# Output stores and residual rows on GpSimd's queue, and the largest magnitude in one reduction, in a gated cross-attention kernel

## The chip, the cores and the metric

The kernel runs on one core of a Trainium2 chip. The metric is the device time of one execution in microseconds (us). Five engines work beside each other, each through its own instructions in order: TensorE (PE, with its weight loads PEld), VectorE (DVE), ScalarE (ACT), GpSimd (POOL) and SyncE (SP), which here only issues transfers. A transfer (DMA) is issued from an engine's queue, and everything behind it in that queue waits until it has been issued.

## The reference

Four stages are applied to x of 2 x 2048 tokens with 512 values each: a cross attention to 128 context rows, a routed block over 256 chosen tokens per batch entry, a second cross attention, and a feed-forward with quantized weights and activations. The change lies in the last:

```python
x = x + jnp.tanh(g_ffn[1]) * _L1_ffn_ref(_layernorm(x, axis=-1), L1_ffn_w1, L1_ffn_conv_w, L1_ffn_conv_b, L1_ffn_w2)

def act_quant(x):
    scale = 127.0 / jnp.clip(jnp.max(jnp.abs(x), axis=-1, keepdims=True), 1e-05)
    return jnp.clip(jnp.round(x * scale), -128, 127) / scale
...
h = bit_linear(x, w1)                             # 512 -> 2048, both sides quantized
h = depthwise_conv1d(h.transpose(0, 2, 1), conv_w, conv_b)   # 3 taps over the tokens
h = jax.nn.silu(h.transpose(0, 2, 1))
return bit_linear(h, w2)                          # 2048 -> 512, both sides quantized
```

The inner rows h need the largest magnitude of each token over all 2048 channels before any of them can be quantized.

## The kernel before, in words

The 4096 tokens are worked on in eight blocks of 512 (`g` from 0 to 7, `LAST` is 7); a block's inner rows are 16 chunks (`HC`) of 128 channels by 512 tokens.

**Stage 3 and the first half.** The second cross attention (`cross_attention`, lines L119 to L131 for the softmax, L253 for queries, L276 scores, L294 and L295 transposes, L302 values, L320 the output product and L329 its addition) runs block after block. When a block is done, `stage3_done` stores its rows (`x3_d`, L1284) and appends two generators to `stream`: `quantize_rows` (integers of the 512 inputs; L90 on POOL gives its normalisation) and `first_half`. `beside4` advances them a few steps beside each of the next block's units. `first_half` works in four groups of four chunks: `convolved` multiplies (L1157), scales (L1167) and convolves a chunk (L1169 on ACT, L1173 twice on DVE). The two columns that the next block needs are copied in and out on POOL (L1166, L1168). Then the group of 128x2048 goes through Silu (L1198), is stored to `h_d` (L1204, SP's queue), and its largest magnitudes are taken: absolute value on ACT in place (L1205), then maxima on DVE (L1206, L1210, L1211, in a block's first group L1206 and L1208). Block 7 is kept on the chip, so its group is not stored, and its absolute values go to a tile of their own (L1202). Blocks 0 to 3 are quantized early (`integers`, L1249 to L1263) and stored as integers in `hq_d`.

**The second half** starts at the end of stage 3 (`second_half_starts`: the weights `w2q`, L1325; integers of blocks 0 and 1; first residual rows). For each block, four tiles of 128 tokens go through `down_and_out`: 16 matmuls into one of four accumulators (L1386), the addition to the residual row tile (L1389, DVE) and the output store (L1390, SP). `row_tile` loads a residual row tile one block ahead (L1316, L1318, SP; eight tiles). `quantize_hidden(g + 1)` runs beside block `g`: for blocks 0 to 3 it loads integers (L1346), for 4 to 6 it loads inner rows (L1353, SP, eight buffers, six chunks ahead), multiplies them by their scale (L1362, DVE) and rounds them on ACT (L1365, L1366) or DVE (L1368). Integer tiles come from two pools, of which the second, `act5`, lies in memory that stage 3 holds until its last product (L320). `last_tokens` handles the final token of each batch entry, whose convolution ends at the border: some small steps and 32 matmuls of one column, called ahead of block 6's rows.

The order of each queue is fixed when the kernel is built, by a scheduler that goes by the order of the program text, ready times and its own estimates; SP's loads, stores and row loads are therefore mixed, but once built their order stands.

Of the kernel before, what the change touches and what calls it, by code (L numbers as in the profile page):

```python
# [10 lines left out]
F32 = mybir.dt.float32  # L11
BF16 = mybir.dt.bfloat16
AF = mybir.ActivationFunctionType
ALU = mybir.AluOpType
AX = mybir.AxisListType
PSUM = bass.MemoryType.PSUM

P = 128
# [3 lines left out]
BLK = 512  # L22
TB = BLK // P
NBLK = S // BLK
# [8 lines left out]
HC = HID // P  # L33
# [10 lines left out]
def flamingo_kernel(ctx: ExitStack, tc: tile.TileContext, a: dict, out: bass.AP):  # L44
    nc = tc.nc
# [697 lines left out]
    with ExitStack() as st:  # L743
# [16 lines left out]
            out=pick,  # L760
            in_=pick,
# [10 lines left out]
            out=after,  # L772
            in_=after,
# [301 lines left out]
    GC = 4  # L1075
# [8 lines left out]
    LAST = B * NBLK - 1  # L1084
# [65 lines left out]
    carry, ending, kept, act5 = {}, [], [], []  # L1150

    def convolved(g, c, z):

        cr = carry[g // NBLK]
        ph = ps_mm.tile([P, BLK], F32, name="ph", tag="mm")
        for d in range(DC):
            nc.tensor.matmul(  # L1157
                ph,
                w1q[:, d, ts(c, P)],
                xiT[g][:, d, :],  # L1160
                start=(d == 0),
                stop=(d == DC - 1),
            )

        u = act4.tile([P, BLK + 2], F32, name="u", tag="u", bufs=3)
        nc.gpsimd.tensor_copy(u[:, 0:2], cr[:, c, :])  # L1166
        nc.vector.tensor_tensor(u[:, 2:], ph, inv_b[g], ALU.mult)  # L1167
        nc.gpsimd.tensor_copy(cr[:, c, :], u[:, BLK:])  # L1168
        nc.scalar.activation(  # L1169
            z, u[:, 1 : BLK + 1], AF.Identity, scale=cw[:, c, 1:2], bias=cb[:, c : c + 1]  # L1170
        )
        for k in (0, 2):
            nc.vector.scalar_tensor_tensor(  # L1173
                z, u[:, ds(k, BLK)], cw[:, c, k : k + 1], z, ALU.mult, ALU.add
            )

    def first_half(g):

        if g % NBLK == 0:

            carry[g // NBLK] = act4.tile([P, HC, 2], F32, name="carry", tag="carry")
            nc.gpsimd.memset(carry[g // NBLK], 0.0)
        amax = act4.tile([P, BLK], F32, name="amax", tag="amax", bufs=1)
        for k in range(HC // GC):
            def hidden(pool, **kw):
                return pool.tile([P, GC, BLK], F32, **kw)

            if g == LAST and k == HC // GC - 1:
                h = hidden(act5[0], name="h7", tag="h7")
            else:  # L1190
                h = hidden(act4, name="h", tag="h", bufs=3)
            if g == LAST:
                kept.append(h)
            for c in range(GC):
                convolved(g, k * GC + c, h[:, c, :])
                if c < GC - 1:
                    yield
            nc.scalar.activation(h, h, AF.Silu)  # L1198

            if g == LAST:  # L1200
                z, h = h, hidden(act5[0], name="ab", tag="ab")
                nc.scalar.activation(h, z, AF.Abs)  # L1202
            else:
                nc.sync.dma_start(out=h_d[g][:, ts(k, GC), :], in_=h)  # L1204
                nc.scalar.activation(h, h, AF.Abs)  # L1205
            nc.vector.tensor_tensor(h[:, 0:2, :], h[:, 0:2, :], h[:, 2:4, :], ALU.max)  # L1206
            if k == 0:
                nc.vector.tensor_tensor(amax, h[:, 0, :], h[:, 1, :], ALU.max)  # L1208
            else:
                nc.vector.tensor_tensor(h[:, 0, :], h[:, 0, :], h[:, 1, :], ALU.max)  # L1210
                nc.vector.tensor_tensor(amax, amax, h[:, 0, :], ALU.max)  # L1211
            yield
        ending.append(scales_of(g, amax))
        if g % NBLK == NBLK - 1:
            b = g // NBLK
            tap = row4.tile([P, HC], F32, name="tap", tag="tap")
            nc.vector.tensor_tensor(tap, carry[b][:, :, 0], cw[:, :, 0], ALU.mult)
            nc.vector.tensor_tensor(z_last[:, b, :], carry[b][:, :, 1], cw[:, :, 1], ALU.mult)
            nc.vector.tensor_tensor(z_last[:, b, :], z_last[:, b, :], tap, ALU.add)
            nc.vector.tensor_tensor(z_last[:, b, :], z_last[:, b, :], cb, ALU.add)  # L1220
# [88 lines left out]
    def row_tile(g, i):  # L1309

        t = w5[0].tile([P, D], F32, name="x5w", tag="x5w", bufs=2)
        if g * TB + i > 1:
            t = act5[0].tile([P, D], F32, name="x5", tag="x5", bufs=8)
        r, p = g % NBLK * BLK + i * P - 1, 0
        if r < 0:
            nc.sync.dma_start(out=t[0:1, :], in_=x3_d[g // NBLK][0:1, :])  # L1316
            r, p = 0, 1
        nc.sync.dma_start(out=t[p:, :], in_=x3_d[g // NBLK][ds(r, P - p), :])  # L1318
        return t, r, p

    def second_half_starts():
# [10 lines left out]
    def quantize_hidden(g):  # L1332

        hq[g] = []

        def integer_tile():

            pool, bufs = (w5[0], 12) if next(next_integers) % 24 < 12 else (act5[0], 12)
            hq[g].append(pool.tile([P, GQ, BLK], BF16, name="hq", tag="hq", bufs=bufs))
            return hq[g][-1]  # L1340

        if g < EARLY:
            for k in range(HC // GQ):
                if g == 1 and k == HC // GQ // 2:
                    yield
                nc.sync.dma_start(out=integer_tile(), in_=hq_d[g][:, ts(k, GQ), :])  # L1346
            return

        def load(c):
            if g == LAST:  # L1350
                return kept[c // GC][:, c % GC, :]
            h = xr.tile([P, D], F32, name="x3", tag="x3")
            nc.sync.dma_start(out=h, in_=h_d[g][:, c, :])  # L1353
            return h

        AHEAD = 6
        hs = [load(c) for c in range(AHEAD)]
        s_b = scales_spread(g)
        yield
        for c in range(HC):  # L1360
            h = hs.pop(0)
            nc.vector.tensor_tensor(h, h, s_b, ALU.mult)  # L1362
            q = (integer_tile() if c % GQ == 0 else hq[g][-1])[:, c % GQ, :]
            if c % 4:
                nc.scalar.activation(h, h, AF.Copy, bias=RND)  # L1365
                nc.scalar.activation(q, h, AF.Copy, bias=-RND)  # L1366
            else:
                nc.vector.tensor_scalar(q, h, RND, RND, ALU.add, ALU.subtract)  # L1368
            if c + AHEAD < HC:
                hs.append(load(c + AHEAD))  # L1370
            if c % 2:
                yield
# [6 lines left out]
    act5.append(s4.enter_context(tc.tile_pool(name="act5", bufs=1)))  # L1379
    w2q = w5[1]  # L1380

    def down_and_out(rows, col, n, t, to, p=0):

        po = ps_5[0].tile([n, D], F32, name="po4", tag="o4")
        for c in range(HC):
            nc.tensor.matmul(  # L1386
                po, rows(c), w2q[:, c, :], start=(c == 0), stop=(c == HC - 1)
            )
        nc.vector.scalar_tensor_tensor(t, po, col, t, ALU.mult, ALU.add)  # L1389
        nc.sync.dma_start(out=to, in_=t[p:, :])  # L1390

    def last_tokens():

# [4 lines left out]
        pm = ps_mm.tile([P, B, P], F32, name="pml", tag="mm")  # L1398
        for b in range(B):
            nc.tensor.transpose(pm[:, b, :], own[:, b : b + 1].to_broadcast([P, P]), ident)  # L1400
        m = row4.tile([P, B], F32, name="ml", tag="lm")
        nc.vector.tensor_reduce(m, pm, AX.X, ALU.max)
        nc.vector.tensor_scalar(m, m, 1e-5, None, ALU.max)
# [7 lines left out]
        for b in range(B):  # L1411
            nc.vector.tensor_scalar(h[:, b, :], h[:, b, :], s[:, b : b + 1], None, ALU.mult)
        nc.vector.tensor_scalar(q, h, RND, RND, ALU.add, ALU.subtract)
        for b in range(B):
            t = act5[0].tile([P, D], F32, name="x5", tag="x5", bufs=8)[0:1, :]
            nc.sync.dma_start(out=t, in_=x3_d[b][S - 1 : S, :])
            down_and_out(
                lambda c: q[:, b, c : c + 1],
                fin[0:1, b : b + 1],
                1,  # L1420
                t,
                out[(b + 1) * S - 1 : (b + 1) * S, :],
            )
# [4 lines left out]
    for g in range(LAST + 1):  # L1428
        if g == LAST - 1:
            while stream or ending:  # L1430
                beside4(None)
            last_tokens()
        behind = quantizing[1] if g == 0 else quantize_hidden(g + 1) if g < LAST else iter(())
        for i in range(TB):
            t, r, p = ahead.pop(0)
            down_and_out(
                lambda c: hq[g][c // GQ][:, c % GQ, ts(i, P)],
                hid_f[:, g * TB + i : g * TB + i + 1],
                P,
                t,  # L1440
                out[ds(g // NBLK * S + r, P - p), :],
                p,
            )
            if g < LAST:
                ahead.append(row_tile(g + 1, i))
            for _ in range(3):
                next(behind, None)
                beside4(None, 1)
# [65 lines left out]
```

## Time and profile before

| | |
|---|---|
| median of 3 runs | 1804.85 us (1802.63 to 1807.84) |
| profiled execution | 1800.29 us, span 1798.6 us |
| mean granted TensorE clock | 0.967 |
| second half, 1600 to 1798.6 us | PE busy 167.7, DVE 145.4, ACT 108.0, POOL 21.3 us |
| stores of inner rows (L1204) | 28 of 1024 KB |
| loads of inner rows in the second half (L1353) | 48 of 256 KB |
| loads of integers (L1346) | 32 of 256 KB |

The profile is taken on one execution. Busy times of an engine are the union of its instructions; a row of costly groups gives a line, its engine, output and inputs, shapes and count, then busy us and mean ns of one, then the engine's idle time just before and what ended most of it. The chain is followed back from the last instruction to whatever released each step.

### The profile page before, as it was taken

To read this page: it belongs to the slowest core of one execution; us is meant where nothing else is said; L and a number is where in the kernel's file an instruction comes from. 1 tells how busy PE (TensorE), PEld (TensorE's weight loads), DVE (VectorE), ACT (ScalarE), POOL (GpSimd) and SP (SyncE) were. 2 spreads that over 40 slices of the span, in tenths; PEclk is the share of its full clock that TensorE was granted. 3 is DMA by queue.
4 is the path that set the end of the run, shared out by engine and by line. 5 is a ranking of instruction groups with operands and counts; after the bars stand their busy time and mean duration, and the time that the engine had idled before them with its cause. 6 is when DMAs were issued, how large, how long until landed. Compare 5 with 4: busy or idle time off the path is not lost.

```text
span 1798.6 us, 25225 instructions
## 1 busy us (share of the span) xinstructions
PE 1648.9 (92%) x8076; PEld 866.4 (48%) x8122; DVE 1282.8 (71%) x2608; ACT 1070.5 (60%) x3106; POOL 537.6 (30%) x671
## 2 busy tenths in 40 slices
PE   6998888989999988999999999999999999888969
PEld 3544444445455655755454544445444454434423
DVE  4676888966767534345358888798798879786967
ACT  2755456445453323435367878788788788744566
POOL 2534443432431012023224242342424324231200
PEclk9999999989889989999999999999999999998989
DMA  6011111121015880730011334234243133256375
GB/s 214 7 65 48 42 60 65 36 88 53 19 42 162 292 268 1 247 86 24 18 54 70 115 100 144 88 126 144 79 150 100 77 115 109 88 187 238 133 237 188
DMA packets 119828, 196.99 MB, mean 110 GB/s; under 512 B 12900, under 2 KB 50532, under 8 KB 115984
## 3 DMA queue, kind: packets, MB, share of 16 engines
q1 hardware_dynamic: 117872, 192.23, 31.2%
q0 software_dynamic: 960, 2.10, 0.6%
q8 instruction: 64, 1.05, 0.2%
q10 hardware_dynamic: 864, 1.05, 0.2%
q14 instruction: 68, 0.56, 0.1%
HBM read 120.89 MB, written 74.45 MB: 109 GB/s over the span
## 4 chain that ended last, share of the span: by engine, by line
PE 56%; DVE 23%; DMA 8%; ACT 6%; POOL 3%; issue 2%; SPq 0%; ACTq 0%; DVEq 0%; POOLq 0%
PE pp L320 14%; PE pq L253 12%; PE po L302 4%; PE sc L276 4%; PE tp L294 4%; PE ph L1157 3%; DVE h L1173 3%; DVE AT L295 2%; ACT A L122 2%; DVE nmx L119 2%; PE po L1386 2%; DVE marks L860 2%; PE pu L646 2%; PE acc L631 2%; PE pw L646 2%
## 5 line engine op out<-in xcount | busy, mean ns | idle before, releaser
L122 ACT ACTIVATE A<-sc,nmx 128x128 f32<-128x128 f32 x1024 | 363.2, 382 | 143.1 <-DVE nmx L119 129.5
L131 POOL TENSOR_TENSOR A<-A,rden 128x512 f32<-128x512 f32 x256 | 277.2, 1085 | 512.4 <-DVE rden L130 402.4
L320 PE MATMUL pp<-L_wo,OT 128*128 128x512 f32 x768 | 367.5, 610 | 16.6 <-DVE x L329 11.2
L253 PE MATMUL pq<-xnT,L_wq 128*128 128x512 f32 x768 | 346.6, 599 | 11.4 <-DVE x L329 11.4
L122 ACT ACTIVATION_READ_ACCUMULATOR A<-sc,nmx 128x1 f32 x1024 | 227.1, 222 | 0.0
L253 PEld LDWEIGHTS pq<-xnT,L_wq 128*128 128x128 f32 x768 | 143.2, 192 | 171.7 <-issue 151.0
L119 DVE TENSOR_REDUCE nmx<-sc 128x4 f32<-128x512 f32 x256 | 168.9, 679 | 69.8 <-PE sc L276 69.8
L320 PEld LDWEIGHTS pp<-L_wo,OT 128*128 128x128 f32 x768 | 136.7, 193 | 162.6 <-issue 132.8
L295 DVE COPY AT<-tp 128x512 f32<-128x512 f32 x256 | 172.9, 680 | 57.8 <-PE tp L294 56.9
L1173 DVE SCALAR_TENSOR_TENSOR h<-u,cw,h 128x512 f32<-128x512 f32 x256 | 204.5, 834 | 5.9 <-ACT h L1169 5.5
L294 PE MATMUL tp<-ident,A 128*128 128x128 f32 x1024 | 164.5, 284 | 25.4 <-POOL A L131 13.9
L294 PEld LDWEIGHTS tp<-ident,A 128*128 128x128 f32 x1024 | 118.2, 143 | 96.4 <-issue 46.0
L276 PEld LDWEIGHTS sc<-L_kT,qT 32*128 32x128 f32 (+1 forms) x2048 | 110.8, 190 | 75.8 <-issue 56.6
L276 PE MATMUL sc<-L_kT,qT 32*128 32x128 f32 (+1 forms) x2048 | 138.2, 292 | 6.5 <-ACT A L122 4.6
L1386 PE MATMUL po<-w2q,hq 128*128 128x512 bf16 x501 | 120.8, 393 | 18.4 <-DVE hq L1368 8.3
L1169 ACT ACTIVATE h<-u,cb,cw 128x512 f32<-128x512 f32 x128 | 99.1, 808 | 64.7 <-DVE u L1167 56.6
L1157 PE MATMUL ph<-xiT,w1q 128*128 128x512 bf16 x477 | 122.3, 379 | 3.8 <-DVE u L1167 1.8
L302 PE MATMUL po<-AT,L_v 128*32 128x512 f32 (+1 forms) x512 | 117.6, 646 | 7.7 <-DVE AT L295 6.2
L1167 DVE TENSOR_TENSOR u<-ph,inv_b 128x512 f32<-128x512 f32 x128 | 85.1, 684 | 31.5 <-PE ph L1157 27.5
L1166 POOL COPY u<-carry 128x2 f32<-128x2 f32 x128 | 49.7, 390 | 166.9 <-DVE h L1173 140.9
L310 ACT COPY OT<-po 128x512 f32<-128x512 f32 x96 | 56.0, 590 | 64.9 <-PE po L302 64.6
L1168 POOL COPY carry<-u 128x2 f32<-128x2 f32 x128 | 48.7, 385 | 149.7 <-DVE u L1167 147.9
(237 smaller groups left out, 2310.2 us busy)
## 6 DMA issues: line engine op xcount, KB each, us to landing
h_d<-h SPq DMA_DIRECT2D x28, 1024.0 KB, 4.4
x_d<-x SPq DMA_DIRECT2D x64, 256.0 KB, 3.2
hf<-h_d SPq DMA_DIRECT2D x64, 256.0 KB, 3.4
x<-x_d SPq DMA_DIRECT2D x61, 256.0 KB, 4.4
x<-h_d SPq DMA_DIRECT2D x48, 256.0 KB, 5.2
x_d<-xo SPq DMA_DIRECT2D x32, 256.0 KB, 2.0
xf<-x_d SPq DMA_DIRECT2D x32, 256.0 KB, 3.5
hq_d<-hi SPq DMA_DIRECT2D x64, 128.0 KB, 1.8
```

The lines of the kernel that those rows point to most:

```text
L119: nc.vector.tensor_reduce(nmx, sc, AX.X, ALU.max, negate=True)
L122: nc.scalar.activation(out_tile[:, h, :], sc[:, h, :], AF.Exp, bias=nmx[:, h : h + 1], accum_out=den[:, h : h + 1],)
L131: nc.gpsimd.tensor_tensor(out_tile, out_tile, rden.unsqueeze(2).to_broadcast([P, n, width]), ALU.mult,)
L253: nc.tensor.matmul(pq, W.wq[:, d, ts(e, P)], xnT[:, d, :], start=(d == 0), stop=(d == DC - 1),)
L276: nc.tensor.matmul(sc[h][:, t, :], qT[e % cpg][r, ts(t, P)], W.kT[r, b, e, :], start=True, stop=True,)
L294: nc.tensor.transpose(tp[:, t, :], A[:, t, :], ident)
L295: nc.vector.tensor_copy(AT, tp.rearrange("p t n -> p (t n)"))
L302: nc.tensor.matmul(po[h * dh : (h + 1) * dh, :], W.v[:, b, ts(hd, dh)], AT[c * hpc + h], start=True, stop=True,)
L320: nc.tensor.matmul(pp, OT[e][:, ts(i, P)], W.wo[:, e, :], start=(e == 0), stop=(e == nE - 1),)
L1157: nc.tensor.matmul(ph, w1q[:, d, ts(c, P)], xiT[g][:, d, :], start=(d == 0), stop=(d == DC - 1),)
L1173: nc.vector.scalar_tensor_tensor(z, u[:, ds(k, BLK)], cw[:, c, k : k + 1], z, ALU.mult, ALU.add)
L1386: nc.tensor.matmul(po, rows(c), w2q[:, c, :], start=(c == 0), stop=(c == HC - 1))
```

## The change

The largest magnitudes of a group are taken by one reduction on DVE over the four chunks, with the absolute value inside the instruction, for all blocks; from the second group of a block on, one maximum with the running value follows. The passes on ACT and the tree of maxima go, and with them the tile `ab`; a small tile `hm` comes. In block 7 the two copies of the carried columns go from POOL to DVE. In the second half the residual rows are loaded, and the output rows of blocks 0 to 6 and of the last tokens stored, from POOL's queue; block 7's stores stay with SP. The pools of integer tiles go from 12 and 12 to 11 and 13. `last_tokens` becomes a generator: its steps follow the row tiles of block 6, its matmuls the fourth of them.

```diff
         u = act4.tile([P, BLK + 2], F32, name="u", tag="u", bufs=3)
-        nc.gpsimd.tensor_copy(u[:, 0:2], cr[:, c, :])
+        carried = nc.vector if g == LAST else nc.gpsimd
+        carried.tensor_copy(u[:, 0:2], cr[:, c, :])
         nc.vector.tensor_tensor(u[:, 2:], ph, inv_b[g], ALU.mult)
-        nc.gpsimd.tensor_copy(cr[:, c, :], u[:, BLK:])
+        carried.tensor_copy(cr[:, c, :], u[:, BLK:])
...
             nc.scalar.activation(h, h, AF.Silu)
-
-            if g == LAST:
-                z, h = h, hidden(act5[0], name="ab", tag="ab")
-                nc.scalar.activation(h, z, AF.Abs)
-            else:
+            if g != LAST:
                 nc.sync.dma_start(out=h_d[g][:, ts(k, GC), :], in_=h)
-                nc.scalar.activation(h, h, AF.Abs)
-            nc.vector.tensor_tensor(h[:, 0:2, :], h[:, 0:2, :], h[:, 2:4, :], ALU.max)
-            if k == 0:
-                nc.vector.tensor_tensor(amax, h[:, 0, :], h[:, 1, :], ALU.max)
-            else:
-                nc.vector.tensor_tensor(h[:, 0, :], h[:, 0, :], h[:, 1, :], ALU.max)
-                nc.vector.tensor_tensor(amax, amax, h[:, 0, :], ALU.max)
+
+            m = amax if k == 0 else act4.tile([P, BLK], F32, name="hm", tag="hm", bufs=1)
+            nc.vector.tensor_reduce(
+                m, h.rearrange("p c n -> p n c"), AX.X, ALU.max, apply_absolute_value=True
+            )
+            if k > 0:
+                nc.vector.tensor_tensor(amax, amax, m, ALU.max)
             yield
...
         if r < 0:
-            nc.sync.dma_start(out=t[0:1, :], in_=x3_d[g // NBLK][0:1, :])
+            nc.gpsimd.dma_start(out=t[0:1, :], in_=x3_d[g // NBLK][0:1, :])
             r, p = 0, 1
-        nc.sync.dma_start(out=t[p:, :], in_=x3_d[g // NBLK][ds(r, P - p), :])
+        nc.gpsimd.dma_start(out=t[p:, :], in_=x3_d[g // NBLK][ds(r, P - p), :])
...
-            pool, bufs = (w5[0], 12) if next(next_integers) % 24 < 12 else (act5[0], 12)
+            pool, bufs = (w5[0], 11) if next(next_integers) % 24 < 11 else (act5[0], 13)
...
-                if g == 1 and k == HC // GQ // 2:
+                if g == 1 and k == 3:
                     yield
...
-    def down_and_out(rows, col, n, t, to, p=0):
+    def down_and_out(rows, col, n, t, to, p=0, queue=nc.gpsimd):
...
-        nc.sync.dma_start(out=to, in_=t[p:, :])
+        queue.dma_start(out=to, in_=t[p:, :])
...
     # last_tokens:
             nc.tensor.transpose(pm[:, b, :], own[:, b : b + 1].to_broadcast([P, P]), ident)
+        yield
...
         nc.vector.tensor_scalar(q, h, RND, RND, ALU.add, ALU.subtract)
+        yield
+        yield
...
         if g == LAST - 1:
             while stream or ending:
                 beside4(None)
-            last_tokens()
+            last = last_tokens()
...
                 p,
+                nc.sync if g == LAST else nc.gpsimd,
             )
             if g < LAST:
                 ahead.append(row_tile(g + 1, i))
+            if g >= LAST - 1:
+                next(last, None)
```

## The prediction

> **What bounds the kernel now.** I read the page first, then the windows, the chain of waits, who waited for whom, and SyncE's own queue.
>
> ```profile
> PE 1648.9 (92%) x8076; PEld 866.4 (48%) x8122; DVE 1282.8 (71%) x2608; ACT 1070.5 (60%) x3106; POOL 537.6 (30%) x671
> 950.00:1600.00 650.00, 617.45 (x2688) 303.27 (x2717) 551.73 (x1005) 511.33 (x1205) 227.92 (x334) 0.99 0.32 112
> 1600.00:1798.60 198.60, 167.69 (x699) 73.27 (x711) 145.43 (x258) 108.04 (x152) 21.29 (x46) 0.92 0.56 196
> 1655.00:1707.00 52.00, 50.48 (x230) 22.85 (x233) 48.24 (x80) 27.63 (x26) 12.13 (x29) 1.00 0.48 170
> ```
>
> The columns of a window are its length, busy PE, PEld, DVE, ACT and POOL, then the granted clock, the DMA share and GB/s. From 950 to 1600 us, where the second cross attention runs beside the first half of the last feed-forward, PE is busy for 617 of 650 us and leaves 32.5; DVE follows with 552 (85%), ACT with 511 (79%). So an ACT pass taken away there is worth little by itself, and DVE has 98 us of room. After 1600 PE leaves 30.9 us of 198.6, at a clock of 0.92. Inside that, 1655 to 1707 is full on both sides: PE idles for 1.5 us and DVE for 3.8.
>
> Who PE waited for after 1600 us (total, times, longest):
>
> ```profile
> PE po L1386 <- DVE hq L1368: 8.3, 2, 8.0
> PE po L1386 <- ACT hq L1366: 6.7, 3, 4.8
> PE pp L320 <- DVE u L1167: 5.4, 1, 5.4
> PE po L1386 <- DMA hq<-hq_d: 2.5, 1, 2.5
> ```
>
> The chain says what stood behind the third:
>
> ```profile
> 1604.25 11.90 DMA h_d<-h
> 1616.23 1.92 ACT h L1205
> 1618.21 1.11 issue
> 1619.32 0.69 DVE u L1167
> 1620.06 8.93 PE pp L320 x16
> ```
>
> The absolute value at L1205 overwrites h, so it waits for the store of h; DVE's maximum waits for ACT, and PE for DVE's next u. Behind the first two stands SyncE's queue (start, length, instruction):
>
> ```profile
> 1669.07 0.38 SPq L1353 DMA_DIRECT2D x<-h_d  x1
> ...
> 1711.37 0.42 SPq L1390 DMA_DIRECT2D out_x<-x  x1
> 1714.86 0.32 SPq L1318 DMA_DIRECT2D x<-x_d  x1
> 1715.28 7.13 SPq L1353 DMA_DIRECT2D x<-h_d  x10
> ```
>
> And what that queue waited for after 1600:
>
> ```profile
> SPq L1390 <- DVE x L1389: 43.8, 20, 8.0
> SPq L1318 <- DMA out_x<-x: 21.2, 12, 6.5
> ```
>
> Inner rows of block 4 are consumed from 1708.9 us (L1362) and the first buffer is free at about 1710.7, but the next load leaves at 1715.28, behind an output store, which waits for DVE, and a residual row, which waits for an older store to land. PE then idles 4.8 us up to 1721.6 and 8.0 us up to 1746.3. Over 1700 to 1750 it idles 16.1 us.
>
> **The change part by part.** The sum is made against the profiled execution, 1800.29 us (span 1798.6 and 1.7 around it); the median of the runs is 1804.85, 4.6 above it.
>
> *The largest magnitude.* It removes 32 ACT passes and the maxima; it adds 32 reductions of 128x2048, read with a step of one chunk (512 values), and 24 maxima of 128x512 (eight of the groups start a block and need none).
>
> ```profile
> L1205 ACT ACTIVATE h<-h 128x2048 f32<-128x2048 f32 x28 | 53.5, 1909 | 26.3 <-DMA h_d<-h 26.3
> L1206 DVE TENSOR_TENSOR h<-h 128x1024 f32<-128x1024 f32 x28 | 34.0, 1216 | 9.5 <-ACT h L1205 9.5
> L119 DVE TENSOR_REDUCE nmx<-sc 128x4 f32<-128x512 f32 x128 | 85.1, 681 | 49.2 <-PE sc L276 49.2
> L131 POOL TENSOR_TENSOR A<-A,rden 128x512 f32<-128x512 f32 x128 | 139.5, 1090 | 276.5 <-DVE rden L130 213.7 <-DVE xqm L1100 11.3 <-PE pp L320 10.3
> ```
>
> DVE pays 1.216 + 0.685 = 1.90 us now in a first group, 1.216 + 2 x 0.685 = 2.59 in the others. 512 to 1024 values cost 0.53 us more, 1.04 ns a value, so a reduction of 2048 read at the rate of L119 is 0.681 + 1536 x 1.04 ns = 2.28 us. No DVE row reads with such a step. For the upper end I take the slowest price per value of an elementwise row, POOL's L131 at 1.09 us for 512: four of them are 4.36 us. At 2.28 a group costs DVE 0.37 us more (2.28 - 1.90, and 2.28 + 0.685 - 2.59); at 4.36, 2.45 more. I take the near row, which is the same instruction on the same engine.
>
> [...]
>
> In stage 3 (28 groups) DVE gains 28 x 0.37 = 10 us of work, in 98 us of room, and one piece of 2.28 in place of 1.2 can delay nmx and AT behind it; ACT loses 53.5 us of work and its waits for stores before 1600 (26.3 less 12.2 after, 14.1). PE waits there mostly for DVE (L329 to L253 9.5 us, AT to L302 6.2, xi to L1141 5.3), so the two nearly cancel: -1 us, between -8 and +8.
>
> *The stall at 1614.7 to 1620.1 us.* With no write to h nothing waits for its store except the next use of the buffer, two groups on. That gives 5.4 us, and the 16 matmuls after it, 8.93 us, come back to the 6.87 that 16 of L253 take: 2.1. Late next is block 0's first integers, already there (L1386 first ran at 1604.5). -7.5 us, between -7.5 and -2.
>
> *Block 7 on DVE.* 32 copies of 128x2 leave POOL. DVE's small steps take 0.09 (L130 in the chain) to 0.2 us (the L1104 to L1106 steps), 3 to 6 us in all, and the four reductions 4 x 0.37 = 1.5. This falls into the full 52 us; nothing covers it. DVE also sheds the wait for POOL (1.8 us for L1168). +5 us, between +2 and +8. At 4.36 us per reduction it is 8 more.
>
> *The queues.* 30 of the 34 output stores (block 7 keeps its four) and 34 row loads move to POOL, which is idle after 1700. An issue there costs POOL 0.6 to 1.0 us (L65, L66 and L968, whose 128 rows are of the same size): 64 x 1.0 us in 170, where POOL was busy 21 after 1600. What queues behind a store that waits for DVE is the next row, due a block (14 us) later, and early on L90 of block 7: three row loads ahead of it would delay it 3 us, beneath the wait of block 1 for its integers.
>
> [...]
>
> SyncE then holds no wait for DVE's L1389 or for older stores. From 1700 to 1750 the most to win is 16.1 us of idle plus two slow stretches (29 matmuls in 8.65 us and 22 in 6.72, against 0.216 each: 4.3), 20 in all. What is late next is the transfer: from 1710 to 1770 the windows moved 15.5 MB (231, 318, 161, 183, 305 and 348 GB/s), which at the 335 of the fuller ones is 46 us of 60, so 14 can come. And quantizing still runs one block ahead over eight buffers. I take 12, between 0 and 20. Block 1's integers, late by 2.5 us, now wait behind less, but one tile more lies in the pool that opens only after L320: 0.
>
> *The last tokens.* Their 32 matmuls (7.07 us from 1758.8) lay just where block 6 waited for its integers (from 1765.8, the last at 1769.8). They now come after block 6's rows. That cover is gone: +4 us, between 0 and +7. Their quantizing before block 6 was hidden.
>
> Sum: -1 - 7.5 + 5 - 12 + 4 = **-11.5**, 1788.8 us on the profiled execution, 1793 on the median.
>
> **The rivals.**
> *Slower: the reduction pays for its step.* At 4.36 us stage 3 has 28 x 2.45 = 69 us more DVE work, 621 of 650 us, level with PE. DVE's 98 us of room can take some; I let half reach PE, +34 (10 to 69) in place of -1, and +8 in block 7: -11.5 + 35 + 8 = +31.5, 1836; with only 10 reaching PE, 1812. For it: no DVE row shows that step, and both engines lie above 85%. Against it: the rate of all DVE rows is about 1 ns a value, in PSUM or SBUF. Each microsecond above 2.28 costs 28 x 0.5 + 4 = 18 us, so it turns slower above about 2.9 us.
> *Nothing gained at the queue.* Transfers, not SyncE, hold blocks 4 to 6, and the tokens' lost cover takes the rest: queues 0, tokens +7, so -1 - 7.5 + 5 + 7 = +3.5, 1808. For it: 318 to 348 GB/s at a share of 0.94 and more; against it: 161 and 183 GB/s from 1730 to 1750.
> *POOL takes SyncE's place.* If POOL's issue holds a row back until after PE's result, L1389 waits and the four accumulators fill: some 3 us in each of four blocks, 1805. Against it: a block of slack.
>
> **How the numbers follow.** About 0.3%, 5.4 us, is what a measurement of this kernel can tell from no change. The forecast (reduction near 2.3 us, queue freed) has 0.48: faster in 0.42, within in 0.05, slower in 0.01. The costly step 0.34: faster 0.04, within 0.02, slower 0.28. No gain at the queue 0.11, POOL 0.07: together faster 0.03, within 0.03, slower 0.12. That gives 0.49, 0.10, 0.41. The forecast's bounds all on one side would give 1771 or 1826; as they will not all fall together, its own range is 1779 to 1808. Signs are mixed, so the range reaches up to the costly step: 1777 to 1837.
>
> **What would show it.** Right: one DVE reduction of 128x2048 near 2.28 us; ACT without L1205 and its 26.3 us; no PE idle before L320 near 1615; L1353 leaving at even distances, and PE idle from 1700 to 1750 below 6 us; POOL busy some 60 us after 1620. Wrong: the reduction above 3 us and DVE above 93% in stage 3; PE waiting for L1362's loads as before; PE idle between blocks 5 and 6.

## The result: 1.3% slower

The changed kernel took 1826.82 us (median of 4 runs, 1823.9 to 1832.44) beside 1803.74 us for the kernel before (4 runs, 1801.02 to 1807.84): a ratio of 1.013 with a 95% interval of 1.010 to 1.016, or 23.5 us at 1805. The prediction said 1793, its range reached to 1837. The profiled execution of after took 1832.44 us, its span is 1830.7.

After's page, the engines' line and the row of the new reduction (count, busy us, mean ns, idle time ahead of it):

```profile
PE 1667.2 (91%) x8122; PEld 873.4 (48%) x8122; DVE 1341.1 (73%) x2608; ACT 1015.3 (55%) x3074; POOL 533.7 (29%) x703
L1204 DVE TENSOR_REDUCE hm<-h 128x512 f32<-128x2048 f32 x24 | 89.0, 3710 | 17.4 <-ACT h L1199 17.4
```

One reduction costs 3.71 us, between the near row's 2.28 and the far row's 4.36. ACT is 55 us lighter, as it should be without its absolute values, but VectorE is 58 us heavier.

After's windows, with the columns of the first windows of the prediction:

```profile
950.00:1600.00 650.00, 607.33 (x2600) 298.32 (x2600) 565.54 (x939) 448.62 (x1147) 193.23 (x310) 0.96 0.29 102
1600.00:1830.70 230.70, 198.97 (x826) 85.50 (x822) 189.20 (x319) 113.26 (x174) 50.94 (x100) 0.95 0.56 196
1700.00:1750.00 50.00, 40.49 (x182) 18.08 (x181) 49.84 (x88) 17.70 (x22) 10.35 (x19) 0.97 0.28 95
```

From 950 to 1600 PE did less than before in the same time: 2600 matmuls in place of 2688 at least (as many as that trace records). It idled 42.7 us in place of 32.5, and it was also slower while busy: the granted clock was 0.96 in place of 0.99, and the 352 matmuls of L253 took 166.3 us in place of 155.3. So the delay consists of waits and of slower matmuls; why the clock was lower no run here shows. 1700 to 1750 is now the stretch of block 7's first half (its pm, L1225, comes at 1744.5 where before had it at 1707.1), and VectorE is busy for 49.84 of 50 us there. Most of the delay is there when the second cross attention ends. Its last output projection, in the PE timeline of before and of after:

```profile
1620.06 8.93 PE L320 MATMUL pp<-L_wo,OT 128*128 128x512 f32 x16 [5.36 <-DVE u L1167]
```

```profile
1658.04 7.03 PE L320 MATMUL pp<-L_wo,OT 128*128 128x512 f32 x16
```

The second line has no wait and takes 7.03 us, about as was forecast when nothing writes h any more. But it ends at 1665.1 and not at 1629.0: 36 us late, where the two profiled executions differ by 32. Not all of it is delay: the scheduler put some 20 matmuls of the second half (L1383, about 5 us) ahead of this pass, where before has 3. What comes behind pm is 5 us shorter than before (86.2 us to the end of the span, 91.5 before).

Who PE waited for from 950 to 1600 us in after (total us, times, longest):

```profile
PE pq L253 <- DVE x L329: 16.9, 5, 6.1
PE pt L1141 <- DVE xi L1135: 7.6, 11, 1.3
...
PE po L302 <- DVE AT L295: 5.0, 8, 1.1
```

From the same window, PE's largest wait in before, then ACT's wait for nmx in before and in after:

```profile
PE pq L253 <- DVE x L329: 9.5, 5, 2.0
ACT A L122 <- DVE nmx L119: 16.1, 16, 2.7
```

```profile
ACT A L122 <- DVE nmx L119: 45.7, 19, 4.9
```

After 1600 us, in after:

```profile
PE po L1383 <- DVE x L1386: 5.1, 1, 5.1
PE ph L1157 <- DVE u L1168: 4.8, 3, 1.9
PE po L1383 <- DMA hq<-hq_d: 4.0, 1, 4.0
PE po L1383 <- DVE hq L1365: 3.8, 3, 2.4
```

The wait of L253 for VectorE's L329 grew from 9.5 to 16.9 us, and its longest from 2.0 to 6.1. After 1600 the waits of 8.0 and 4.8 us for a block's integers are gone; the longest for integers is 4.0. ACT shows the delay inside a chain of attention: its L122, the exponentials, waits for VectorE's nmx 45.7 us in 950 to 1600, where before had 16.1.

The queues behaved as the diff says. What SyncE and then GpSimd waited for after 1600 us in after:

```profile
SPq L1350 <- DVE hq L1365: 61.3, 5, 55.2
...
SPq L1350 <- ACT hq L1363: 18.1, 17, 2.7
```

```profile
POOL x L1315 <- DMA out_x<-x: 65.2, 19, 5.9
POOL out_x L1387 <- DVE x L1386: 32.8, 8, 9.5
```

SyncE's timeline shows that no store and no row stands any more between 44 of the 48 loads of inner rows:

```profile
1690.13 100.77 SPq L1350 DMA_DIRECT2D x<-h_d  x44
```

The waits for L1386 and for landings, 65 us on SyncE before, are 98 us on GpSimd now. By these views one half of the change did what it should and the other cost more than the first brought; the experiments take them apart.

### The profile page after: what moved, and what is told of

Its sections match the earlier page's. It is cut to its first block, busy times and chain, and to the rows that moved or that the text cites. A ratio compares the mean times of both kernels' runs of the same rounds, so it can differ in the third digit from the quotient of the medians.

```text
span 1830.7 us, 25204 instructions
## 1 busy us (share of the span) xinstructions
PE 1667.2 (91%) x8122; PEld 873.4 (48%) x8122; DVE 1341.1 (73%) x2608; ACT 1015.3 (55%) x3074; POOL 533.7 (29%) x703
## 4 chain that ended last, share of the span: by engine, by line
PE 24%; DVE 20%; ACT 7%; issue 3%; DMA 3%; POOL 1%; SPq 0%; ACTq 0%; DVEq 0%; POOLq 0%
PE pp L320 6%; PE pq L253 6%; DVE h L1174 4%; DVE hm L1204 3%; PE po L302 3%; PE ph L1157 2%; PE po L1383 2%; ACT A L122 2%; DVE u L1168 2%; PE sc L276 2%; PE tp L294 2%; DVE AT L295 1%; DVE nmx L119 1%; ACT h L1199 1%; DMA x<-h_d 1%
## 5 line engine op out<-in xcount | busy, mean ns | idle before, releaser
L122 ACT ACTIVATE A<-sc,nmx 128x128 f32<-128x128 f32 x1024 | 363.1, 382 | 171.9 <-DVE nmx L119 154.3
L320 PE MATMUL pp<-L_wo,OT 128*128 128x512 f32 x768 | 367.7, 608 | 14.8 <-DVE x L329 14.8
L253 PE MATMUL pq<-xnT,L_wq 128*128 128x512 f32 x768 | 358.6, 616 | 21.7 <-DVE x L329 19.6
L253 PEld LDWEIGHTS pq<-xnT,L_wq 128*128 128x128 f32 x768 | 146.9, 197 | 189.6 <-issue 159.0
L122 ACT ACTIVATION_READ_ACCUMULATOR A<-sc,nmx 128x1 f32 x1024 | 226.8, 221 | 0.0
L320 PEld LDWEIGHTS pp<-L_wo,OT 128*128 128x128 f32 x768 | 135.9, 192 | 161.6 <-issue 133.2
L119 DVE TENSOR_REDUCE nmx<-sc 128x4 f32<-128x512 f32 x256 | 168.7, 678 | 56.4 <-PE sc L276 56.3
L1174 DVE SCALAR_TENSOR_TENSOR h<-u,cw,h 128x512 f32<-128x512 f32 x256 | 197.1, 804 | 5.8 <-ACT h L1170 5.2
L276 PEld LDWEIGHTS sc<-L_kT,qT 32*128 32x128 f32 (+1 forms) x2048 | 114.6, 190 | 75.1 <-issue 56.9
L276 PE MATMUL sc<-L_kT,qT 32*128 32x128 f32 (+1 forms) x2048 | 143.3, 292 | 5.4 <-ACT A L122 3.7
L1383 PE MATMUL po<-w2q,hq 128*128 128x512 bf16 x512 | 121.9, 390 | 16.0 <-DVE x L1386 5.1
L1204 DVE TENSOR_REDUCE hm<-h 128x512 f32<-128x2048 f32 x24 | 89.0, 3710 | 17.4 <-ACT h L1199 17.4
L1168 DVE TENSOR_TENSOR u<-ph,inv_b 128x512 f32<-128x512 f32 x128 | 84.7, 681 | 23.4 <-PE ph L1157 21.8
L1167 POOL COPY u<-carry 128x2 f32<-128x2 f32 x112 | 39.8, 357 | 180.9 <-DVE h L1174 158.7
```

The costliest lines, as they stand in the source:

```text
L119: nc.vector.tensor_reduce(nmx, sc, AX.X, ALU.max, negate=True)
L122: nc.scalar.activation(out_tile[:, h, :], sc[:, h, :], AF.Exp, bias=nmx[:, h : h + 1], accum_out=den[:, h : h + 1],)
L253: nc.tensor.matmul(pq, W.wq[:, d, ts(e, P)], xnT[:, d, :], start=(d == 0), stop=(d == DC - 1),)
L276: nc.tensor.matmul(sc[h][:, t, :], qT[e % cpg][r, ts(t, P)], W.kT[r, b, e, :], start=True, stop=True,)
L320: nc.tensor.matmul(pp, OT[e][:, ts(i, P)], W.wo[:, e, :], start=(e == 0), stop=(e == nE - 1),)
L1174: nc.vector.scalar_tensor_tensor(z, u[:, ds(k, BLK)], cw[:, c, k : k + 1], z, ALU.mult, ALU.add)
```

## The experiments

Two theories stood at the start. A: the reduction's reads with a step of 512 values cost the time (1.4 us a group over the price of the sum), and the queues bring what they were meant to. B: the queues, the late tokens or block 7's copies on VectorE cost it. All ratios are to before on the same chip, with 95% intervals; microseconds are the ratio less one, times 1805. Line numbers move by up to four between kernels.

**The two halves apart.** First the queues, copies and tokens with the old magnitude (the integer pools, 11 and 13 or 12 and 12, go with the magnitude in both halves):

```diff
 # after, with before's step back
+            nc.scalar.activation(h, h, AF.Abs)
+            nc.vector.tensor_tensor(h[:, 0:2, :], h[:, 0:2, :], h[:, 2:4, :], ALU.max)
...
-            nc.vector.tensor_reduce(m, h.rearrange("p c n -> p n c"), ...)
```

> The changed kernel with the magnitudes taken as before (absolute value on ACT in place, three maxima on DVE) and the integer pools at 12 and 12; queues, carried columns and last tokens as changed. Theory A (the reduction's price, 3.72 us with its step, is what costs): DVE loses 3.72 - 1.90 = 1.82 us a group against the changed kernel, 51 us in stage 3 and 7 in block 7, and the time falls to 1790-1800 us, below the kernel before. Theory B (the queues on GpSimd cost): it stays at 1820 or more. Theory C (any change of the scheduled order costs some 10 us): 1810-1820.

Measured: 1789.51 us, ratio 0.9905 (0.9884 to 0.9926), -17.1 us. Then the reduction alone in before:

```diff
 # before, with after's step
-            nc.scalar.activation(h, h, AF.Abs)
...
+            nc.vector.tensor_reduce(m, h.rearrange("p c n -> p n c"), ...)
```

> The kernel before with the one reduction (and the integer pools at 11 and 13); queues, carried columns and last tokens as before. Theory A: nearly the whole loss or more, 1825-1840 us, last L320 at about 1665 us. Theory B: 1800-1810, as before. Theory C: 1810-1820.

Measured: 1843.87 us, ratio 1.021 (1.019 to 1.0229), +37.9 us, a little above the 1825 to 1840 us expected. The two add up to +20.8, beside after's +23.5 (18 to 29). B falls: the queues' half is a clear gain, and queues_only beats both kernels.

**The read step.** The same reduction, over four neighbouring values in place of four chunks. Other values are compared, the work is the same:

```diff
-                m, h.rearrange("p c n -> p n c"), AX.X, ALU.max, apply_absolute_value=True
+                m, h.rearrange("p c n -> p (c n)").rearrange("p (n c) -> p n c", c=GC), AX.X, ...
```

> The changed kernel whose reduction reads groups of four neighbouring values instead of one value from each of four chunks: same instruction, same number of values in and out, step 1 (its magnitudes, and so the output, are not those of the reference). Theory A with the step as the cause: the reduction takes 2.28 us, DVE loses 1.44 x 32 = 46 us, and the time is 1790-1800. Rival (the size or the groups of four make it slow): it takes 3.7 us and the time stays at 1820-1830. Rival (the price does not matter, only that one long instruction blocks DVE): 2.28 us but 1815 or more.

Measured: 1798.48 us, ratio 0.9951 (0.993 to 0.9971), -8.8 us. Its page has the reduction at the price of the prediction's near row, to 3 ns:

```profile
L1204 DVE TENSOR_REDUCE hm<-h 128x512 f32<-128x2048 f32 x24 | 54.7, 2277 | 6.4 <-ACT h L1199 6.4
```

The step alone is thus worth 23.5 + 8.8 = 32 us, for 1.43 us on each of 32 reductions (46 us of work), and it turns the sign. The order did not change with it: in the two traces the instructions of each engine stand in the same order, line by line. In this kernel the last L320 pass, and matmuls of the second half ahead of it, lie here in the PE timeline:

```profile
1606.09 3.83 PE L1383 MATMUL po<-w2q,hq 128*128 128x512 bf16 x17
1621.10 1.24 PE L1383 MATMUL po<-w2q,hq 128*128 128x512 bf16 x5
1631.94 7.03 PE L320 MATMUL pp<-L_wo,OT 128*128 128x512 f32 x16
```

It ends at 1639.0, 10 us later than before, where VectorE has 28 x 0.37 = 10 us more to do in stage 3. But some 5 of these 10 us are the 22 matmuls shown, so about half of VectorE's work arrives there.

**Without any such read.** Running maxima over the four chunks, the absolute value left out:

```diff
-            nc.vector.tensor_reduce(m, h.rearrange("p c n -> p n c"), ...)
...
+            for c in range(GC):
...
+                nc.vector.tensor_tensor(amax, first, h[:, c, :], ALU.max)
```

> The changed kernel with four running maxima of 128x512 in place of the reduction (three in a block's first group), without the absolute value (left out, so a token whose largest magnitude is negative is scaled otherwise). 4 x 0.685 = 2.74 us a group against 3.72 + 0.685 = 4.41. Theory A: 1785-1800 us. Rival (one ACT pass and its wait fewer is what the changed kernel lives from, DVE's work does not matter): 1820-1830.

Measured: 1797.96 us, ratio 0.9949 (0.993 to 0.9968). Its row of maxima:

```profile
L1207 DVE TENSOR_TENSOR amax<-amax,h 128x512 f32<-128x512 f32 x112 | 80.1, 715 | 12.6 <-ACT h L1199 11.6
```

At 715 ns each they cost 2.86 us a group, close to the 2.28 + 0.685 of the last kernel, and so is the time. That agrees with the microseconds on VectorE being what counts, not the kind of instruction.

**Where the step begins to cost.** The reduction by itself on one tile, at seven steps:

```diff
+        nc.vector.tensor_reduce(
+            r.rearrange("p (a s) -> p a s", s=step),
+            h.rearrange("p (a c s) -> p a s c", c=4, s=step), AX.X, ALU.max, ...)
```

> Most of the computation is left out: one tile of 128x2048 is loaded, and VectorE makes the same reduction of 2048 values to 512 six times for each of the read steps 1, 2, 4, 8, 16, 128 and 512 values (4 to 2048 bytes), once more at 512 without the absolute value, and beside it a copy of 2048 values in order and one that reads with step 512. [...] Rival (the distance itself costs, or a bank): still rising above step 16. Rival (the reduction's change of order costs, not the address): 3.7 us already at step 2. [...]

Its groups, six instructions each (the names tell the step in values; by_chunk and in_order are the copies):

```profile
L66 DVE TENSOR_REDUCE step_four<-h 128x512 f32<-128x2048 f32 x6 | 22.6, 3773 | 0.0
L73 DVE TENSOR_REDUCE step_eight<-h 128x512 f32<-128x2048 f32 x6 | 22.6, 3773 | 0.0
...
L94 DVE TENSOR_REDUCE step_chunk<-h 128x512 f32<-128x2048 f32 x6 | 21.8, 3626 | 0.0
L101 DVE TENSOR_REDUCE plain_chunk<-h 128x512 f32<-128x2048 f32 x6 | 21.8, 3626 | 0.0
L80 DVE TENSOR_REDUCE step_sixteen<-h 128x512 f32<-128x2048 f32 x6 | 21.5, 3582 | 0.0
L52 DVE TENSOR_REDUCE step_one<-h 128x512 f32<-128x2048 f32 x6 | 13.7, 2277 | 5.5 <-DMA h<-in_x 5.5
L59 DVE TENSOR_REDUCE step_two<-h 128x512 f32<-128x2048 f32 x6 | 13.7, 2275 | 0.0
L107 DVE TENSOR_SCALAR by_chunk<-h 128x2048 f32<-128x2048 f32 x6 | 12.2, 2025 | 0.0
...
L112 DVE TENSOR_SCALAR in_order<-h 128x2048 f32<-128x2048 f32 x6 | 7.4, 1226 | 0.2
```

Here a step of 8 bytes was free (2,275 ns beside 2,277 in order), one of 16 bytes took 1.66 times as long (3,773), and beyond that distance changed little (3.58 to 3.77 us). The absolute value cost nothing (3,626 ns with it and without, plain_chunk). The copy pays too, by 1.65 (2.03 us with the step, 1.23 in order). The rival of distance falls, and so does that of the changed order, since step two has it as well and is free.

**Which part of the queues' half brings the gain.** Four single parts of queues_only put back as they were:

```diff
 # q_tokens_up_front
             last = last_tokens()
+            for _ in last:
+                pass
 # q_copies_gpsimd
-        carried = nc.vector if g == LAST else nc.gpsimd
+        carried = nc.gpsimd
 # q_rows_sync: residual rows
-        nc.gpsimd.dma_start(out=t[p:, :], ...)
+        nc.sync.dma_start(out=t[p:, :], ...)
 # q_stores_sync: output stores
-    def down_and_out(rows, col, n, t, to, p=0, queue=nc.gpsimd):
+    def down_and_out(rows, col, n, t, to, p=0, queue=nc.sync):
```

> The queues-only kernel (1789.5 us in its own comparison), with the last tokens' 32 matmuls made before block 6, as before. Theory of the prediction (their place before block 6 covered the wait for its integers, and losing that cover costs 4 us, 0 to 7): about 1785.5 us, and fewer microseconds of PE idle between blocks 5 and 6. Rival (with SyncE freed block 6's integers are there in time, so the tokens' matmuls cover nothing in either place): 1789.5 within 2 us. Second rival (made up front, their chain ACT, DVE, PE holds PE up, and leaving it for later is part of the gain): 1792 us or more.

> The queues-only kernel with block 7's carried copies back on GpSimd. Theory of the prediction (32 copies on VectorE cost 3 to 6 us in a stretch full on both sides, less 1.8 us of waits for GpSimd): 1786 us, and the L1168 to pm stretch of block 7 3 us shorter. Rival (GpSimd now issues the row loads and stores that wait for VectorE and for landings, and the copies stand behind them in its order): slower than 1789.5 by 5 to 20 us, VectorE waiting for GpSimd's u for more than 5 us in all.

> The queues-only kernel with the residual rows back on SyncE; the stores stay on GpSimd. Theory that the stores' waits for VectorE (43.8 of the 65 us that SyncE waited) were what held the inner rows: most of the gain stays, 1793 us, at most 1796. Rival (the rows wait for stores to land, 21.2 us on SyncE before, and one wait ahead of the inner rows is enough): 1799 us or more, PE idle in 1700 to 1750 us above 8 us.

> The queues-only kernel with the output stores back on SyncE; the residual rows stay on GpSimd. Theory that the stores' waits for VectorE held the inner rows: most of the gain goes, 1801 us or more, inner row loads behind stores again and PE idle in 1700 to 1750 us above 10 us. Rival (the rows with their waits for landings were what held SyncE): 1793 us or less.

| put back | median us | ratio to before | us |
|---|---|---|---|
| nothing (queues_only, earlier) | 1789.51 | 0.9905 (0.9884 to 0.9926) | -17.1 |
| tokens up front | 1792.73 | 0.9922 (0.9896 to 0.9949) | -14.1 |
| copies on GpSimd | 1786.47 | 0.9888 (0.9857 to 0.9918) | -20.2 |
| rows on SyncE | 1791.01 | 0.9931 (0.9904 to 0.9957) | -12.5 |
| stores on SyncE | 1792.33 | 0.9927 (0.99 to 0.9954) | -13.2 |

No single part carries it, and all four intervals overlap that of queues_only; the rival by which copies on GpSimd cost 5 to 20 us is refuted. My theory of the stores (moving them back takes most of the gain) is wrong by the time, and so is its mirror image: the waits on SyncE after 1600 us are still there in sum, in the kernel with the rows and then in that with the stores:

```profile
SPq L1319 <- DMA out_x<-x: 47.9, 15, 8.0
```

```profile
SPq L1391 <- DVE x L1390: 56.8, 25, 7.5
```

Either kind alone may wait 50 us on SyncE and costs 4 to 5 us by the medians of the ratios. That left a doubt whether the queues matter at all, which two more kernels settled: both kinds back on SyncE with tokens and copies as changed, and the two queue moves alone.

```diff
 # q_all_sync: queues_only with
-        nc.gpsimd.dma_start(out=t[p:, :], ...)
+        nc.sync.dma_start(out=t[p:, :], ...)
-    def down_and_out(rows, col, n, t, to, p=0, queue=nc.gpsimd):
+    def down_and_out(rows, col, n, t, to, p=0, queue=nc.sync):
 # queues_alone: queues_only with
+            for _ in last:
+                pass
-        carried = nc.vector if g == LAST else nc.gpsimd
+        carried = nc.gpsimd
```

> The queues-only kernel with the residual rows and the output stores both on SyncE again; block 7's copies on VectorE and the last tokens made late stay. It has the old magnitude, so it is before with these two small parts alone. Theory (SyncE held the inner rows whenever either a store or a row stood ahead of them, so moving either is nearly enough): 1803 us or more, PE busy in 1700 to 1750 us about 34 us as in before. Rival (the gain comes from making the last tokens late or from the copies, since undoing either queue alone kept three quarters of it): below 1797 us.

> Before with the two moves of the queues alone: residual rows and output stores on GpSimd, the carried copies on GpSimd and the last tokens up front as before. Theory (the two moves carry the whole gain, and the tokens and the copies are worth 3 us either way at most): 1786 to 1792 us. Rival (the late tokens or the copies bring a third of it or more): 1796 us or more.

Measured: q_all_sync 1807.41 us, ratio 1.002 (1.0005 to 1.0035), +3.6 us; queues_alone 1788.47 us, ratio 0.9908 (0.9888 to 0.9928), -16.6 us. The two moves carry the whole gain. Windows of q_all_sync and then of queues_alone:

```profile
1600.00:1650.00 50.00, 39.85 (x135) 17.10 (x137) 34.93 (x65) 21.80 (x21) 7.58 (x14) 0.92 0.48 177
1700.00:1750.00 50.00, 32.69 (x143) 14.32 (x144) 30.29 (x66) 25.34 (x42) 0.00 (x0) 0.84 0.62 205
```

```profile
1600.00:1650.00 50.00, 45.06 (x158) 20.08 (x160) 42.59 (x74) 27.34 (x27) 17.75 (x33) 0.95 0.73 265
1700.00:1750.00 50.00, 44.76 (x206) 18.79 (x208) 42.78 (x83) 39.13 (x68) 11.48 (x21) 1.00 0.88 290
```

PE is busy 5.2 us more in the first stretch and 12.1 more in the second, 17.3 together, where the two profiled executions differ by 15.6 us. Before has 33.88 in the second. With the rows alone on SyncE, and then with the stores alone:

```profile
1600.00:1650.00 50.00, 43.23 (x149) 18.70 (x151) 37.05 (x68) 24.21 (x24) 10.60 (x19) 0.93 0.61 226
1700.00:1750.00 50.00, 42.88 (x194) 17.80 (x196) 41.56 (x82) 37.84 (x67) 5.94 (x11) 1.00 0.89 309
```

```profile
1600.00:1650.00 50.00, 45.38 (x167) 20.70 (x169) 39.48 (x72) 27.71 (x28) 14.36 (x26) 0.93 0.65 229
1700.00:1750.00 50.00, 38.75 (x172) 16.69 (x173) 36.99 (x74) 31.93 (x57) 4.92 (x9) 0.90 0.81 271
```

So the stores alone do bring a stall back (PE idles 11.2 us in the second stretch, as the theory of the stores said, where queues_alone has 5.2), but the first stretch keeps its gain. From q_all_sync to queues_alone the DMA share rises from 0.62 to 0.88 in the second stretch: transfers that waited in a queue now run, and PE's granted clock is 1.00 there in place of 0.84. Most of the cost comes only with the pair on one queue. The traces show one place of it: in SyncE's timelines four loads of inner rows leave before 1670 us, and the next one at 1718.4 us with both on SyncE, at 1711.2 with the rows, at 1705.7 with the stores. That the rows wait for stores that are themselves held on the same queue, behind inner rows, would explain the pair; it is argued and no run shows it.

**Shorter pieces.** After, with the reduction in four instructions:

```diff
-            nc.vector.tensor_reduce(m, h.rearrange("p c n -> p n c"), ...)
+            for i in range(TB):
+                nc.vector.tensor_reduce(m[:, ts(i, P)], h[:, :, ts(i, P)].rearrange("p c n -> p n c"), ...)
```

> After with each group's reduction made in four pieces of 128x512 to 128x128, one behind the other, still reading with a step of 512 values; nothing else changed. The work on VectorE grows a little (four times the fixed part of some 0.15 us, less what the pipeline hides: about 1.0 us a piece, 4.0 a group where one took 3.72). Theory that the amount of work on VectorE is what reaches TensorE (51 us more of it in stage 3 moved the last L320 by 36): 1832 us, 1827 to 1838, the last L320 start some 5 us later than 1664.5. Rival (one long piece in VectorE's order delays nmx, AT and u of the other chain, and shorter pieces let them in between): below 1820 us, the wait of ACT's L122 for nmx in 950 to 1600 us well below the 45.7 us of after.

Measured: 1836.59 us, ratio 1.0162 (1.0148 to 1.0176), +29.2 us; ACT's L122 waits 49.4 us for nmx. The rival (below 1820) falls. The pieces, in a block's later groups:

```profile
L1205 DVE TENSOR_REDUCE hm<-h 128x128 f32<-128x512 f32 x96 | 93.2, 1032 | 16.9 <-ACT h L1199 16.8
```

A piece spans 1.03 us, but the spans overlap: VectorE is busy 93.2 / 24 = 3.88 us a group, where one reduction took 3.71. That is 28 x 0.17 = 5 us more work in stage 3. The last L320 pass comes 2.4 us later than in after, where I had expected 5, and the time is 6 us longer, with intervals that overlap. So the length of a piece did not matter here, and the amount of work is not contradicted. But in VectorE's order the four pieces follow each other with nothing between them, so what pieces spread among other work would do stays open.

## Why the prediction was wrong, step by step

*The price of the reduction: the step that failed.* The sum took 2.28 us from the near row, L119, because it is the same instruction on the same engine. L119 reads in order, and reduce_step_one shows that its rate is exact for reading in order (2,277 ns). With a step of 512 values the instruction measured 3.71. The far row, 4.36, was nearer. The evidence "the rate of all DVE rows is about 1 ns a value" (in before from 0.4 in L727, 422 ns for 1024, to 1.6 in L1173, 834 for 512) came only from rows that read in order; it held no information on the step. In steps_alone the same instruction took 2,275 ns with a step of 8 bytes and 3,773 with one of 16: the factor is 1.66 at most, where the far row has 4.36 / 2.28 = 1.91.

*How much of it reaches PE.* The rival let half of VectorE's extra work through, for 98 us of room and an 85% share. Measured, 32 us of time came for 32 x 1.43 = 46 us of work, 0.7 of it. The last L320 pass says 0.6 (36 us less the 5 of reordered matmuls, for 28 x 1.82 = 51 us). The sign that I named for it, VectorE above 93%, never came (565.5 of 650 is 87%): idle time that lies between steps which others wait for was no room here. The whole price is 32 us for 1.43, 22.6 us for each microsecond where the prediction had 18, and the turning point is 2.28 + 8.8 / 22.6 = 2.7 us where it had 2.9. At 3.71 its own formula gives -11.5 + 18 x 1.43 = +14; the rival named the right mechanism and sign, with its size 9 us short.

*Stage 3 and the stall at 1614.7 us.* At the price assumed, the forecast had -1 for stage 3, -7.5 for the stall and +1.5 for the reductions of block 7, -7 in all. Measured, with the queues moved in both: reduce_step_one less queues_only, -8.8 + 17.1 = +8.3. Neither of these two kernels has the stall, so 7.5 of the 15 us between forecast and measurement are the stall's, credited to the wrong half. The other 8 lie in the two other terms, +0.5 in the forecast (-1 and +1.5): most of VectorE's 12 us of additional work reached the end, and the lighter ACT did not cancel it. The stall does go when nothing writes h, as forecast, but it also goes in queues_only, which still writes h:

```profile
1621.19 7.03 PE L320 MATMUL pp<-L_wo,OT 128*128 128x512 f32 x16
```

And in q_all_sync it is there as before (6.39 us). In queues_only the pass ends at 1628.2, 0.8 earlier than before, so little comes back at L320 itself; PE is busy 5 us more from 1600 to 1650.

*The queues.* -12 was forecast, between 0 and -20; queues_alone measured -16.6 (-20.2 to -13.0), which includes what the stall was worth (PE is busy some 5 us more from 1600 to 1650). The place was right: PE idle from 1700 to 1750 falls from 16.1 to 5.2 us in queues_alone, where "below 6" was the sign. In after the signs are shifted out of that window by the 37 us. The rivals "nothing gained at the queue" and "POOL takes SyncE's place" are refuted by the same run. An issue cost GpSimd 0.55 us in after (median of L1315 and L1387, 0.50 to 0.71), not 1.0.

*Tokens and copies.* +4 and +3.5 were forecast. Together they measured +3.6 (0.9 to 6.3) on the old queues and -0.5 on the moved ones (-17.1 beside -16.6), so with SyncE freed the cover that was "gone" was no longer needed. The 32 copies took 0.16 to 0.17 us each on VectorE, 5.2 us in all, as the prediction assumed, but that work did not show in the time clear of the noise. Putting the copies alone back gave 3 us and the tokens alone cost 3, each within the intervals.

Summed with these numbers: -16.6 for the queues, 0 for tokens and copies, +8 for the reduction read in order and +32 for its step make +23.4, and after stands at +23.5. The last two terms are differences to after's halves, so the sum has to close; the test from outside is magnitude_only, +37.9 beside 8 + 32 = 40. The forecast's -11.5 would have been off by 3 us if the reduction had cost 2.28, since its two other errors, 15 one way and 12 the other, nearly cancelled. That would have been luck: a total that comes out well is no proof of its terms.

## What to carry to other kernels

Before costing an instruction from a row of the same kind, compare how the two walk through memory: here a row that reads in order (L119, its rate good for 2.28 us) said nothing about one that reads with a step of a chunk (3.71), and where no row has the step, the forecast should stand between the two ends and not on the near one. Idle time of an engine that others wait for in short turns was no room here: about 0.7 of each microsecond added to a VectorE that was 85% busy arrived at the end. And judge a queue by the waits on it together: here taking either kind off kept three quarters of the gain, so try the halves and not only the whole.

## What the runs showed of the hardware

In steps_alone VectorE's reduction of 128x2048 float32 values took 2.28 us at steps of 4 and 8 bytes, and 3.58 to 3.77 us at 16 bytes and beyond, up to 2 KB. A copy of 128x2048 float32 values there, 1.23 us in order, took 2.03 us with a step of 2 KB on its input. The factors are close, 1.57 to 1.66 and 1.65, though the copy ran at nearly twice the reduction's rate. PE's granted clock differed with the queue: 0.84 from 1700 to 1750 us in q_all_sync, where PE was busy for 32.7 us, 1.00 in queues_alone, where it was busy for 44.8.
